# Attention kernel: 256-column q and k products issued one at a time between 512-column products

## The chip, the cores and the metric

The kernel runs on one core of one Trainium2 chip. The metric is the device time of one execution in microseconds (us); the time of a kernel is the median of several runs. The engines are named as the profile names them: PE is TensorE's matmul, PEld its weight load, DVE is VectorE, ACT is ScalarE, POOL is GpSimd, SP is SyncE.

## The reference, cut to what matters

```python
# x: (4, 64, 64, 256); Wq, Wk: (256, 128); Wv: (256, 256); gamma: one number
q = einsum('bwhc,cd->bwhd', x, Wq) + bq
k = einsum('bwhc,cd->bwhd', x, Wk) + bk
v = einsum('bwhc,cd->bwhd', x, Wv) + bv
pq, pk, pv = q.reshape(B, -1, N), k.reshape(B, -1, N), v.reshape(B, -1, N)   # N = 4096
energy = einsum('bcn,bcm->bnm', pq, pk)          # contraction over 128
attention = softmax(energy, axis=-1)
out = einsum('bcm,bnm->bcn', pv, attention)
return gamma * out.reshape(B, W, H, C) + x
```

For each of the 4 images there are 4096 positions; the score matrix is 4096 x 4096 and is never kept whole.

## The kernel before, in words

All products are float32. To keep precision at the rate of single products, each operand is split into a rounded upper part `h`, a rest `l` and a combination `d`, and each exact product is made of three matmuls over these forms (form numbers 0, 1 and 2; 2 is `d`). Every matmul here has 128 stationary columns and streams 512 or 256 moving columns.

**The main loop** (`for n in range(B * STEPS)`) takes 512 units of work, 128 for each image: 8 groups of 512 output columns by 16 steps over the keys. One unit issues, in this order of the program, which is also the order on each engine (the schedule is written by hand):

1. `cross(n + LOOK)`: two matmuls of form 2 into the two score banks (L378), each followed on ACT by a scaling in place (L379).
2. `step(p, "act")`: ACT's share of the preparation of the next image.
3. `attend(n, 0)`: six matmuls (L452) that add v times attention to the first half's two accumulators: two with `h`, two with `l`, two with `d`.
4. `energy(n + LOOK)`: four matmuls (L393), two for each score bank, each pair followed on ACT by an exponential (L396).
5. `load_k`, `store`, and `upper` on ACT (L402).
6. `step(p, "pe")`: PE's share of the preparation of the next image.
7. `halves(n + 1)` on DVE: the running sum (L413), then `l` (L428) and `d` (L430) of the next unit; then `step(p, "dve")`: DVE's share of the preparation.
8. `attend(n, 1)`: six matmuls (L452) for the second half.

So a unit has 18 matmuls of 512 columns on PE, and those of the preparation when the unit has some.

**The preparation of the next image** (`step`, images 1 to 3) goes in periods of R = 16 units. Each period makes q, k and v of two blocks of 256 positions, `i` and `i + 1`, at the place `r` in the period:

- r = 1, 2 (DVE): each block of x is transposed into a spare PSUM bank (p0 or p1).
- r = 3, 4 (ACT, then DVE, L165): the transposed block's `h`, then `d` (tile `xd`) and `l` (tile `xf`). The `l` is the last reader of the bank.
- r = 5 (PE, L267): `products(b, i, 0, (2,))` and the same for `i + 1`, 4 + 4 matmuls of 256 columns with `xd`, into p0 and p1. Then DVE scales these banks and adds the bias (`seed_qk`, L295).
- r = 6 (PE, L267): `products(b, i, 0, (0, 1))` and the same for `i + 1`, 8 + 8 matmuls of 256 columns with `xf`.
- r = 7, 8 (ACT, L317) and r = 7 to 10 (DVE, L320): the forms of q and k of `i`, then of `i + 1`, stored to DRAM.
- r = 9 to 14: the same for v, in products of 512 columns (`products_v`, L284), which take p0 at r = 9 and p1 at r = 11.

There are 8 periods in each of images 1 to 3, so 24 in all; in image 0 the products are made ahead of the main loop, by the same function.

Of the kernel before, what the change touches and what calls it, by code (L numbers as in the profile page):

```python
# [20 lines left out]
def kernel(  # L21
# [79 lines left out]
    with ExitStack() as fast:  # L101
# [41 lines left out]
        nc.gpsimd.dma_start(gam, gamma.partition_broadcast(P))  # L143

        qd, kf, vf, units, loads, now = {}, {}, {}, {}, {}, {}
        active, stores, xloads = [], [], []

        def proceed():
            for pieces in list(active):
# [38 lines left out]
        def bank(name, shape, b, ring):  # L188
            if b:
                tile_ = spare(name, shape)  # L190
                now["turn"] += 1
                return tile_
            pool, tag = next(rings[ring])
            return pool.tile(shape, F32, tag=tag, name=name)
# [52 lines left out]
            units["xf", b, i] = f  # L247
            yield from split(*f, y, b == 0 and i > 1)

        def products(b, i, w, fs):  # L250

            xf = units["xf", b, i]
            if fs[0] == 2:
                ring = 1
                if b == 0 and w and i >= NI - 2:
                    ring = 0
                    next(rings[1])
                units[w, b, i] = bank(f"qv{w}_{b}_{i}", [P, 2, C], b, ring)
            to = units[w, b, i]
            for s in range(2):  # L260
                for f in fs:
                    for k in range(KC):
                        if w:
                            left, right = wf[:, 1, f, k, s * P : (s + 1) * P], xf[f][:, k]
                        else:
                            left, right = xf[f][:, k, s, :], wf[:, 0, f, k]
                        nc.tensor.matmul(  # L267
                            to[:, s, :],
                            left,
                            right.rearrange("p s a -> p (s a)") if w else right,  # L270
                            start=(f == 2 and s == k == 0),
                            stop=(f == 1 and k == KC - 1),
                            skip_group_check=True,
                        )

        def products_v(b, i, eh, fs):

# [15 lines left out]
        def seed_qk(b, i):  # L293
            y = units[0, b, i]
            nc.vector.scalar_tensor_tensor(  # L295
                y, y, REST, bias.unsqueeze(1).to_broadcast([P, 2, C]), ALU.mult, ALU.add
            )
# [8 lines left out]
        def seed_v_pair(b, i, eh):  # L306
            y = units["v", b, i, eh]
            nc.scalar.activation(y, y, AF.Identity, bias=bvs[:, eh : eh + 1], scale=REST)
# [52 lines left out]
        def load_k(n):  # L361
            b, u = divmod(n, STEPS)
            if b < B:
                t = kpool.tile([P, 2, 3, P], F32R, tag="k", name=f"k_{b}_{u}")
                nc.gpsimd.dma_start(t, kf[b, u % NU])  # L365
                loads["k", n] = t

        def forms(n, i, f):
            b, u = divmod(n, STEPS)
            return loads["k", n][:, i, f, :], loads["q", b, u // NU][:, :, f, :]  # L370

        def cross(n):

            if n >= B * STEPS:
                return
            for i in range(2):
                e = units["e", n, i] = ps_e.tile([P, NB], F32, tag="e", name=f"e_{n}_{i}")
                nc.tensor.matmul(e, *forms(n, i, 2), start=True, stop=False, skip_group_check=True)  # L378
                nc.scalar.mul(e, e, -REST)  # L379

        def energy(n):

            if n >= B * STEPS:
                return
            if n % NU:
                x = ppool.tile([P, 2, NB], F32, tag="x", name=f"x_{n}")
            else:
                x = ppool.tile([P, 2, NB], F32, tag="s", name=f"s_{n // NU}")
            units[n] = x
            for i in range(2):  # L390
                e = units.pop(("e", n, i))
                for f in range(2):
                    nc.tensor.matmul(  # L393
                        e, *forms(n, i, f), start=False, stop=(f == 1), skip_group_check=True
                    )
                nc.scalar.activation(x[:, i, :], e, AF.Exp, scale=(1.0 + E) ** 3 / E)  # L396

        def upper(n):
# [41 lines left out]
        def attend(n, j, order=(0, 1, 2)):  # L440

            t = n % NU
            if t == 0:
                for i, c in enumerate("ab"):
                    pool, tag = ps_o, f"{c}{j}"
                    if j and n >= (B - 1) * STEPS and n // NU % 2 == 0:
                        pool, tag = now["banks"][i]
                    now[c, j] = pool.tile([P, NB], F32, tag=tag, name=f"{c}{j}_{n // NU}")
            for f in order:
                to = now["ab"[f == 2], j]  # L450
                for i in (1, 0) if f == 1 else (0, 1):
                    nc.tensor.matmul(  # L452
                        to,
                        vall[:, t, i, f, j * P : (j + 1) * P],
                        units[n][f][:, i, :],
                        start=(t == 0 and i == 0 and f != 1),
                        stop=(t == NU - 1 and f != 0 and i == f // 2),
                        skip_group_check=True,
                    )

        def emptied(n, j, banks=None, only=None, vector=False):

# [100 lines left out]
        def step(n, engine):  # L563

            if n < 0:
                return
            b, u = divmod(n, STEPS)
            i, r = divmod(u, R)
            b, i = b + 1, 2 * i
            if b >= B:  # L570
                return
            made = now["made"]

            def begin(key, pieces):
                made[key] = pieces
                next(pieces)

            if engine == "pe":
                if r == 5:
                    products(b, i, 0, (2,))  # L580
                    products(b, i + 1, 0, (2,))
                elif r == 6:
                    products(b, i, 0, (0, 1))
                    products(b, i + 1, 0, (0, 1))
                elif r in (9, 11):
                    products_v(b, i, r // 11, (2,))
                elif r in (10, 12):
                    products_v(b, i, r // 12, (0, 1))
            elif engine == "act":
                if r in (3, 4):  # L590
                    begin(("x", r - 3), x_forms(b, i + r - 3))
                elif r in (7, 8):
                    begin(("qk", r - 7), qk_forms(b, i + r - 7))
                elif r in (10, 12):
                    seed_v_pair(b, i, r // 12)
                    if r == 12:
                        load_x(b + (i + 2) // NI, (i + 2) % NI)
                elif r in (11, 13):
                    begin(("v", r // 13), v_pair_forms(b, i, r // 13))
            else:  # L600
                if r in (1, 2):
                    transposed(b, i + r - 1)
                elif r in (3, 4):
                    next(made["x", r - 3])
                    next(made["x", r - 3])
                elif r == 5:
                    seed_qk(b, i)
                    seed_qk(b, i + 1)
                elif 7 <= r <= 10:
                    next(made["qk", (r - 7) // 2])  # L610
                    if r % 2 == 0:
                        next(made["qk", (r - 7) // 2], None)
                elif 11 <= r <= 14:
                    next(made["v", (r - 11) // 2])
                    if r % 2 == 0:
                        next(made["v", (r - 11) // 2], None)
# [84 lines left out]
        for n in range(B * STEPS):  # L701
            b, u = divmod(n, STEPS)
# [7 lines left out]
            if n == B * STEPS - 6:  # L710
                xr = ppool.tile([P, 2, NB], F32, tag="s", name="xr")
                nc.sync.dma_start(xr, xg[b, g])
            cross(n + LOOK)
            turn = t == NU - 1 and not final
            if t == 0 and n:
                upper(n + LOOK - 1)
            p = n - 2 + (n > 17)
            step(p, "act")
            late = n >= (B - 1) * STEPS
            if not final:  # L720
                attend(n, 0)
            if late and 1 <= t <= 2 and n > 1:
                emptied(n - 1 - t, 1, done, t - 1)
            energy(n + LOOK)
            load_k(n + LOOK + 3)
            store()
            if t == 0 and n:
# [22 lines left out]
            for m in range(2 * NU):  # L750
                c, r = divmod(n + NU - 3 - 13 * m // 16, STEPS)
# [11 lines left out]
    with tc.If(nc.values_load(again[0:1, 0:1]) > 0), ExitStack() as general:  # L763
# [91 lines left out]
        for b in range(B):  # L855
# [16 lines left out]
            for g in range(NG):  # L872
                ps = []
                mx = work.tile([P, 2, NB], F32, tag="mx", name=f"gmx_{b}_{g}")
                for t in range(NP):
# [9 lines left out]
                    p = ppool.tile([P, 2, NB], F32, tag="p", name=f"gp_{b}_{g}_{t}")  # L885
# [52 lines left out]
                r = work.tile([P, NB], F32, tag="r", name=f"gr_{b}_{g}")  # L938
# [36 lines left out]
```

## Time and profile before

| | |
|---|---|
| median of 3 runs | 2300.16 us (2299.88 to 2301.19) |
| the profiled execution's own time | 2299.82 us |
| span in the profile, first to last instruction | 2298.0 us |
| mean granted TensorE clock | 0.999 |
| PE busy | 2286.8 us, 10566 matmuls |
| DVE busy | 2160.6 us |
| ACT busy | 1794.3 us |
| 256-column products in images 1 to 3 | 576 (192 with `xd`, 384 with `xf`) |

The profiled execution lies 0.34 us below the median of the runs, and 1.8 us of it lie outside the span. In the rows of a timeline the columns are the start in us from the span's start, the length in us, engine, line, operation, output and inputs, and how many equal instructions were merged. A matmul's length includes the way through the array, and matmuls overlap; what one of them costs PE is the distance from its start to the start of the next.

### The profile page before, as it was taken

The page shows a single profiled execution, that of the slowest core. Times are in us where ns is not written, and L with a number is a line of the kernel's source. Part 1 is how long each engine was busy: PE and PEld are TensorE (multiplying, and loading weights), DVE is VectorE, ACT ScalarE, POOL GpSimd, SP SyncE. Part 2 cuts the span into 40 slices and gives each one's busy share as a digit, 9 for nine tenths or more (in the row PEclk, how much of TensorE's full clock was granted, in tenths as well). Part 3 has the DMA queues.
Part 4 walks back from the last instruction along what each step waited for, and adds up shares of the span by engine and source line. Part 5 has one row for each costly group of instructions (what it writes and reads, how often), then busy time and mean ns, then how long its engine had stood idle before and what let it go on. Part 6 is the DMA issues. An engine that isn't in the chain of part 4 may idle for free.

```text
span 2298.0 us, 31903 instructions
## 1 busy us (share of the span) xinstructions
PE 2286.8 (100%) x10566; PEld 1912.7 (83%) x10566; DVE 2160.6 (94%) x2222; ACT 1794.3 (78%) x2917; POOL 445.3 (19%) x747
## 2 busy tenths in 40 slices
PE   9999999999999999999999999999999999999998
PEld 9888888888888888888888888888888888888886
DVE  8999999999999999999999999999999899888888
ACT  7778777787777877777777778777788777888885
POOL 7111111111231111111122111111112211111110
PEclk9999999999999999999999999999999999999999
DMA  8567766677996777666799667766689855555554
GB/s 272 161 172 212 195 180 165 174 210 194 279 278 194 196 195 192 181 167 184 209 301 278 180 178 206 199 177 170 169 228 299 243 148 144 136 137 146 151 142 107
DMA packets 305727, 445.31 MB, mean 194 GB/s; under 512 B 129682, under 2 KB 183188, under 8 KB 305556
## 3 DMA queue, kind: packets, MB, share of 16 engines
q0 software_dynamic: 105584, 296.79, 49.5%
q1 hardware_dynamic: 199424, 146.14, 20.6%
q8 instruction: 87, 1.43, 0.3%
q14 instruction: 84, 0.69, 0.1%
q10 hardware_dynamic: 548, 0.26, 0.0%
HBM read 313.79 MB, written 112.26 MB: 185 GB/s over the span
## 4 chain that ended last, share of the span: by engine, by line
PE 99%; DVE 0%; ACT 0%; DMA 0%; issue 0%; DVEq 0%
PE a L452 40%; PE e L393 20%; PE b L452 20%; PE e L378 10%; PE qv L267 5%; PE v L284 3%; PE xt L229 0%; DMA xs<-in_x_dram 0%; ACT qv L302 0%; DVE ld L430 0%; PE wp L140 0%; PE zp L525 0%; DVE o_last L555 0%; DVE o_last L550 0%; DVE o_last L556 0%
## 5 line engine op out<-in xcount | busy, mean ns | idle before, releaser
L396 ACT ACTIVATE x<-e 128x512 f32<-128x512 f32 x960 | 522.0, 596 | 324.1 <-PE e L393 324.1
L379 ACT ACTIVATE e<-e 128x512 f32<-128x512 f32 x1024 | 546.3, 570 | 114.8 <-PE e L378 114.8
L452 PE MATMUL a<-h,v 128*128 128x512 f32 x2048 | 631.3, 389 | 0.0
L452 PE MATMUL b<-ld,v 128*128 128x512 f32 x2048 | 631.0, 389 | 0.1
L452 PE MATMUL a<-ld,v 128*128 128x512 f32 x2048 | 630.9, 389 | 0.0
L413 DVE TENSOR_TENSOR s<-s,x 128x1024 f32<-128x1024 f32 x480 | 585.2, 1219 | 48.3 <-ACT x L396 46.7
L365 POOL DMA_DIRECT2D k<-kf x512 | 273.0, 533 | 1799.9 <-PE e L393 1750.1
L428 DVE TENSOR_TENSOR ld<-x,h 128x1024 fp32r<-128x1024 f32 x480 | 585.6, 1220 | 22.6 <-ACT h L402 22.2
L430 DVE SCALAR_TENSOR_TENSOR ld<-h,x 128x1024 fp32r<-128x1024 f32 x480 | 585.8, 1220 | 0.0
L393 PE MATMUL e<-q,k 128*128 128x512 f32 x2048 | 547.6, 389 | 0.0
L402 ACT ACTIVATE h<-x 128x1024 fp32r<-128x1024 f32 x480 | 510.8, 1064 | 14.2
L452 PEld LDWEIGHTS b<-ld,v 128*128 128x128 f32 x2048 | 384.2, 188 | 80.9 <-DVE ld L430 1.1
L452 PEld LDWEIGHTS a<-ld,v 128*128 128x128 f32 x2048 | 384.5, 188 | 80.3
L393 PEld LDWEIGHTS e<-q,k 128*128 128x128 f32 x2048 | 384.4, 188 | 79.6
L452 PEld LDWEIGHTS a<-h,v 128*128 128x128 f32 x2048 | 381.4, 188 | 75.9
L378 PE MATMUL e<-q,k 128*128 128x512 f32 x1024 | 315.4, 389 | 0.0
L378 PEld LDWEIGHTS e<-q,k 128*128 128x128 f32 x1024 | 192.0, 188 | 39.9
L320 DVE SCALAR_TENSOR_TENSOR f<-f,qv 128x512 fp32r<-128x512 f32 x128 | 86.2, 684 | 0.3
L267 PE MATMUL qv<-wf,xf 128*128 128x256 f32 x576 | 77.2, 285 | 0.6 <-DVE qv L295 0.4
L267 PEld LDWEIGHTS qv<-wf,xf 128*128 128x128 f32 x576 | 73.7, 191 | 3.6 <-DVE qv L295 0.6
L428 DVE TENSOR_TENSOR ld<-s,h 128x1024 fp32r<-128x1024 f32 x32 | 39.3, 1227 | 37.0 <-ACT h L402 34.4
L165 DVE SCALAR_TENSOR_TENSOR vf<-vf,v 128x512 fp32r<-128x512 f32 x96 | 65.6, 683 | 0.0
(87 smaller groups left out, 1100.3 us busy)
## 6 DMA issues: line engine op xcount, KB each, us to landing
k<-kf POOLq DMA_DIRECT2D x512, 384.0 KB, 3.7
vf<-vf SPq DMA_DIRECT2D x96, 384.0 KB, 4.8
v<-vf POOLq DMA_DIRECT2D x96, 384.0 KB, 6.0
kf<-f SPq DMA_DIRECT2D x128, 192.0 KB, 3.9
qd<-f SPq DMA_DIRECT2D x124, 192.0 KB, 3.9
q<-qd POOLq DMA_DIRECT2D x31, 768.0 KB, 5.2
o<-o POOLq DMA_DIRECT2D x31, 512.0 KB, 5.3
o<-in_x_dram POOLq DMA_DIRECT2D x31, 512.0 KB, 6.8
```

The costliest lines, as they stand in the source:

```text
L267: nc.tensor.matmul(to[:, s, :], left, right.rearrange("p s a -> p (s a)") if w else right, start=(f == 2 and s == k == 0), stop=(f == 1 an ...
L320: nc.vector.scalar_tensor_tensor(f[:, :, :, j, :], h.bitcast(F32), s, y, ALU.mult, op)
L365: nc.gpsimd.dma_start(t, kf[b, u % NU])
L378: nc.tensor.matmul(e, *forms(n, i, 2), start=True, stop=False, skip_group_check=True)
L379: nc.scalar.mul(e, e, -REST)
L393: nc.tensor.matmul(e, *forms(n, i, f), start=False, stop=(f == 1), skip_group_check=True)
L396: nc.scalar.activation(x[:, i, :], e, AF.Exp, scale=(1.0 + E) ** 3 / E)
L402: nc.scalar.activation(h, units[n], AF.Identity, scale=UPPER)
L413: nc.vector.tensor_tensor(s, s, x, ALU.add)
L428: nc.vector.tensor_tensor(l, x, h.bitcast(F32), ALU.subtract)
L430: nc.vector.scalar_tensor_tensor(d, h.bitcast(F32), 1.0 + E, x, ALU.mult, ALU.subtract)
L452: nc.tensor.matmul(to, vall[:, t, i, f, j * P : (j + 1) * P], units[n][f][:, i, :], start=(t == 0 and i == 0 and f != 1), stop=(t == NU - ...
```

## The change

The function `products` becomes a generator, `each_product`, that yields after each matmul. A list `between` holds generators that wait to be emitted; `mix()` emits one matmul of the first of them, and `flush()` all that are left. `mix()` is called after each matmul of `cross` and `energy`, and after each of `attend` except the two with `h` of the first half.

The 8 products with `xd` at r = 5 are put on the list ahead of `attend(n, 0)` (a new engine name, "first"): 4 fall between the `l` and `d` matmuls of `attend(n, 0)`, 4 between those of `energy`. The 8 products of block `i` with `xf` are put on the list at r = 6, after `energy`, and fall between the 6 matmuls of `attend(n, 1)` and the 2 of the next unit's `cross`. The 8 of block `i + 1` do the same at r = 7, one unit later than before. `flush()` stands after `cross` and after `energy`. Image 0's products keep their runs. The other engines' instructions keep their order.

```diff
+        def mix():
+            while between:
+                if next(between[0], None) is None:
+                    del between[0]
+                else:
+                    return
+
+        def flush():
+            while between:
+                mix()
+
+        def products(*which):
+            for _ in each_product(*which):
+                pass
+
-        def products(b, i, w, fs):
+        def each_product(b, i, w, fs):
...
                             skip_group_check=True,
                         )
+                        yield True
...
                 nc.tensor.matmul(e, *forms(n, i, 2), start=True, stop=False, skip_group_check=True)
+                mix()
                 nc.scalar.mul(e, e, -REST)
...
                         e, *forms(n, i, f), start=False, stop=(f == 1), skip_group_check=True
                     )
+                    mix()
...
                         stop=(t == NU - 1 and f != 0 and i == f // 2),
                         skip_group_check=True,
                     )
+                    if j or f:
+                        mix()
...
-            if engine == "pe":
+            if engine == "first":
                 if r == 5:
-                    products(b, i, 0, (2,))
-                    products(b, i + 1, 0, (2,))
-                elif r == 6:
-                    products(b, i, 0, (0, 1))
-                    products(b, i + 1, 0, (0, 1))
+                    between.append(each_product(b, i, 0, (2,)))
+                    between.append(each_product(b, i + 1, 0, (2,)))
+            elif engine == "pe":
+                if r in (6, 7):
+                    between.append(each_product(b, i + r - 6, 0, (0, 1)))
...
             cross(n + LOOK)
+            flush()
...
             if not final:
+                step(p, "first")
                 attend(n, 0)
...
             energy(n + LOOK)
+            flush()
```

More of the change, by code (lines that the diff above doesn't have):

```diff
@@ L145 @@
         qd, kf, vf, units, loads, now = {}, {}, {}, {}, {}, {}
-        active, stores, xloads = [], [], []
+        active, stores, xloads, between = [], [], [], []
         def proceed():
```

## The prediction

> **What bounds the kernel now.** I read the page first: busy times, then the chain that ended last.
>
> ```profile
> span 2298.0 us, 31903 instructions
> PE 2286.8 (100%) x10566; PEld 1912.7 (83%) x10566; DVE 2160.6 (94%) x2222; ACT 1794.3 (78%) x2917; POOL 445.3 (19%) x747
> ...
> PE 99%; DVE 0%; ACT 0%; DMA 0%; issue 0%; DVEq 0%
> ```
>
> PE is the chain: 99% of the span is one matmul after another. A busy PE need not be an efficient one, so the next question is how far apart the matmuls start. The waits of PE come next, all that the view lists:
>
> ```profile
> engine line waited for: us in total, times, longest us
> PE wp L140 <- DVE ones L132: 1.1, 1, 1.1
> PE qv L267 <- DVE qv L295: 0.4, 1, 0.4
> PE xt L229 <- DMA xs<-in_x_dram: 0.3, 1, 0.3
> PE qv L267 <- ACT qv L302: 0.2, 1, 0.2
> ```
>
> They come to 2.0 us and stand at the beginning. There is nothing to win from waits: only a matmul's own cost counts, and any new wait of PE adds to the time in full.
>
> Then PE's timeline over one period's products (r = 5 to 8), where a start minus the start before it is what the matmuls between them cost:
>
> ```profile
> start us, us, engine line op out<-in xcount [idle before <-releaser]
> ...
> 799.43 0.62 PE L452 MATMUL a<-h,v 128*128 128x512 f32 x2
> ...
> 800.79 1.07 PE L393 MATMUL e<-q,k 128*128 128x512 f32 x4
> 801.70 1.11 PE L267 MATMUL qv<-wf,xd 128*128 128x256 f32 x8
> 802.65 0.63 PE L452 MATMUL a<-h,v 128*128 128x512 f32 x2
> 803.12 0.62 PE L452 MATMUL a<-ld,v 128*128 128x512 f32 x2
> 803.58 0.62 PE L452 MATMUL b<-ld,v 128*128 128x512 f32 x2
> 804.03 0.61 PE L378 MATMUL e<-q,k 128*128 128x512 f32 x2
> 804.49 0.62 PE L452 MATMUL a<-h,v 128*128 128x512 f32 x2
> ...
> 806.75 2.08 PE L267 MATMUL qv<-wf,xf 128*128 128x256 f32 x16
> 808.67 0.63 PE L452 MATMUL a<-h,v 128*128 128x512 f32 x2
> ...
> 810.51 0.62 PE L452 MATMUL a<-h,v 128*128 128x512 f32 x2
> ...
> 814.59 0.62 PE L452 MATMUL a<-h,v 128*128 128x512 f32 x2
> ```
>
> The unit from 810.51 to 814.59 has no 256-column product: 4.08 us for 18 matmuls, **226.7 ns** each. The unit at 799.43 has 8 and takes 5.06 us, so they cost 0.98 us; the one at 804.49 has 16 and takes 6.02 us, so 1.94 us. The difference, 0.96 us for 8, gives **120 ns** for one more product in a run. Half a 512-column matmul would be 113.3 ns. The rest, 0.98 - 8 x 0.12 = 0.02 us, is paid once a run, and the rows show where: the matmuls after the run start 0.47, 0.46, 0.45 us apart by pairs instead of 0.453, and the eight from 802.65 to 804.49 take 1.84 us instead of 1.813. The two runs of a period cost 2.92 us for 24 products, **121.7 ns** each.
>
> The same timeline at single points inside the first run (the first row of each answer is the matmul then running, merged with the next):
>
> ```profile
> 801.70 0.40 PE L267 MATMUL qv<-wf,xd 128*128 128x256 f32 x2
> ```
>
> ```profile
> 801.81 0.40 PE L267 MATMUL qv<-wf,xd 128*128 128x256 f32 x2
> ```
>
> ```profile
> 801.93 0.40 PE L267 MATMUL qv<-wf,xd 128*128 128x256 f32 x2
> ```
>
> The first product, the one that follows a 512-column matmul, costs 0.11 us; the others (0.95 - 0.11) / 7 = 0.12 us. So the price grows inside the run: the second product already finds PE behind. The weight loads say the same from the other side, in the groups of lines L267 and L452 from 70 us on (lengths in ns: least, median, most):
>
> ```profile
> L267 PEld LDWEIGHTS qv<-wf,xf x384: 187/192/192, 101.4 to 1730.4; 128*128 128x128 f32 x192
> L267 PE MATMUL qv<-wf,xf x384: 277/283/283, 101.6 to 1730.5; 128*128 128x256 f32 x192
> L267 PEld LDWEIGHTS qv<-wf,xd x192: 187/192/192, 96.4 to 1724.4; 128*128 128x128 f32 x192
> ```
>
> ```profile
> L452 PEld LDWEIGHTS a<-ld,v x2042: 187/188/188, 71.7 to 2288.5; 128*128 128x128 f32 x186
> ```
>
> A load between 512-column matmuls takes 187 to 188 ns; in a run of 256-column ones its median is 192. Loads crowd in the runs and not elsewhere. Their own rate is not shown anywhere, so that a run is held up by them is my reading, not a measurement.
>
> **The change part by part.** *Removed:* 48 runs in 24 periods, 24 x 2.92 = 70.1 us. *Added:* the same 576 products (384 + 192 in the rows), each between two 512-column matmuls. The trace has no such place, so the price is bounded. From below: half of a 512-column matmul, 113.3 ns, with which the first product of a run agrees (0.11). From above: a run's price of 120 ns and the whole 0.02 us that returning to 512 columns costs, 140 ns. I take 113.3, the row nearest to the new place: that first product also follows a 512-column matmul, and whatever follows it needs a weight load of the same size. Then 576 x 113.3 ns = 65.3 us, and the sum is 65.3 - 70.1 = **-4.8 us**. I count no tail after a single product, since the second product of a run starts on time and the crowding shows only from then on.
>
> *The Trainium skill* would have it otherwise. "TensorE: Matmul & The Clock Gate", section "Back-to-back issue gap", gives a warm matmul a gap of N / 2.4 + 2.5 ns, and section "LDWEIGHTS (loading the stationary operand)" gives 106.7 ns for 128 columns, less than that gap for N = 256 (109.2). By it a run is not held up by loads, and an estimate from that page would leave nothing for the change to remove. The trace disagrees with the gap itself (226.7 ns against 215.8 for 512 columns, 120 against 109.2 for 256), so I keep the rows, and its sense as a rival below.
>
> *Moved, r = 5:* the `xd` products go ahead, past half of `attend(n, 0)`. PE is in order, so whatever such a product waits for holds up the scores and the sums behind it. The fourth product of `i` is done before `energy`; the first of `i + 1` comes after the first `energy` matmul and needs the bank that `xf`'s `l` form reads last. DVE's timeline there, and around the next unit but one:
>
> ```profile
> 797.66 1.22 DVE L430 SCALAR_TENSOR_TENSOR ld<-h,x 128x1024 fp32r<-128x1024 f32 x1
> 798.79 0.68 DVE L165 SCALAR_TENSOR_TENSOR xd<-xf,xt 128x512 fp32r<-128x512 f32 x1
> 799.39 0.68 DVE L165 SCALAR_TENSOR_TENSOR xf<-xf,xt 128x512 fp32r<-128x512 f32 x1
> ...
> 802.26 1.22 DVE L430 SCALAR_TENSOR_TENSOR ld<-h,x 128x1024 fp32r<-128x1024 f32 x1
> ```
>
> ```profile
> 808.70 1.22 DVE L430 SCALAR_TENSOR_TENSOR ld<-h,x 128x1024 fp32r<-128x1024 f32 x1
> ```
>
> The `l` is done at 800.07. PE comes to that product at 799.43 + 7 x 0.2267 + 4 x 0.1133 = 801.47: 1.4 us to spare. Without that cover the price would be the lateness itself, once a period.
>
> *Moved, r = 6 and 7:* 8 products leave r = 6, so unit r = 7 starts its `attend(n, 0)` about 1 us earlier: at 799.43 + 2 x (18 x 0.2267 + 8 x 0.1133) = 809.40 instead of 810.51. Its first `d` matmul comes four later, at 810.31; DVE's `d` is done at 808.70 + 1.22 = 809.92. The slack shrinks from 1.5 to 0.4 us and holds: nothing. If it did not, each 0.1 us would be 2.4 us over 24 periods. The bias on p0 and p1 (L295) comes behind the 802.26 row on DVE, after 803.48, when the products are long done. Block `i + 1` ends in the next `cross`, just ahead of ACT's reading of it at r = 8, where ACT first has the two scalings to do, 570 ns each:
>
> ```profile
> L379 ACT ACTIVATE e<-e 128x512 f32<-128x512 f32 x1024 | 546.3, 570 | 114.8 <-PE e L378 114.8
> ```
>
> A product behind the second `cross` matmul takes 0.11 us, within them. The DMA issues, SP's and POOL's queues keep their order; the stores of `i + 1` hang on the forms at r = 9 and 10, as before. Nothing.
>
> *The first period* is different: there DVE is late already.
>
> ```profile
> 94.34 0.61 PE L452 MATMUL a<-ld,v 128*128 128x512 f32 x2
> 95.09 0.73 PE L452 MATMUL b<-ld,v 128*128 128x512 f32 x2
> ```
>
> ```profile
> 93.80 1.23 DVE L430 SCALAR_TENSOR_TENSOR ld<-h,x 128x1024 fp32r<-128x1024 f32 x1
> ...
> 95.53 0.69 DVE L165 SCALAR_TENSOR_TENSOR xf<-xf,xt 128x512 fp32r<-128x512 f32 x1
> ```
>
> PE stands 0.3 us for `d` (95.09 - 94.34 - 2 x 0.2267), into which two products now fit (-0.2 us); the bank of `i + 1` is read until 96.22 and wanted at 95.09 + 3 x 0.2267 + 2 x 0.1133 = 96.00 (+0.2 us). Together nothing.
>
> So 2299.82 - 4.8 = 2295.0 us for an execution like the profiled one, which lies 0.34 us under the median of the runs: **2295.4 us** expected.
>
> **The rivals.**
>
> *The price goes with the instruction, not with its neighbours.* 226.7 - 120 = 106.7 ns for 256 columns more: taken so, each matmul has a fixed 13.3 ns, and 120 is what a 256-column one costs anywhere. For it: two rows fit with one constant, and the skill's rule above has this form. Against it: the first product's 0.11. Only the 48 x 0.02 us go: -1.0 us, 2299.2 us. The same comes out if a single product costs 113.3 and the 512-column one behind it 6.7 more.
>
> *The return to 512 columns is paid each time: slower.* The 0.02 us come after 8 as after 16 products, so a single one may cost them in full. Place: the first 512-column matmuls behind each product; price 140 ns, 576 x (140 - 121.7) = +10.6 us, 2310.8 us. It decides from 121.7 ns a product on, that is if more than 8 of the 20 ns, added to 113.3, come with each single one. For it: the slower matmuls go on over 1.8 us behind a run, longer than the distance between two single products. Against it: they follow runs in which PE has fallen behind. Half of it would be about 2301.
>
> *DVE's `d` at r = 7 is late.* With 0.4 us used up, each 0.2 us beyond is 4.8 us and cancels the gain: 2300. Against it: DVE waits for nothing new.
>
> *The change doesn't come about* can be left out: with 6 + 2 and 4 + 4 places for 8 products, nothing is left for `flush()` to issue in a run.
>
> **How the numbers follow.** Single products at 113 ns or a little less: 0.48. Its -4.8 us is just past 0.2% (4.6 us), which is about what a measurement of this kernel can tell from no change; I give 0.34 to faster, since the first product's 0.11 allows a price under 113.3 too, and 0.14 to no change. The fixed price, and the gain cancelled by late DVE: 0.26, no change. The paid return: 0.26, of it 0.21 slower and 0.05 no change. So faster 0.34, no change 0.45, slower 0.21. The range goes from 2293.5 (110 ns a product, the first one's 0.11 taken as it stands: 576 x 11.6 ns = 6.7 us under 2300.16) to 2306.0 (132 ns a product, most of a paid return). It takes in the fixed price and the cancelled gain; left out are the full return, about 0.14, and less than 110 ns, 0.04.
>
> **What would show it.** Right: in the profile after, an `attend` with products between its matmuls advances by 0.34 us for each pair (226.7 + 113.3); the units at r = 5, 6 and 7 take 4.99 us each; the loads of L282 (L267 before) drop to 188 ns. If the pairs take 0.347 us, the price is fixed; if 0.36, the return is paid, and the rows behind show it. A wait of PE for DVE at r = 5 or 7, some 20 times, would show a slack that I misjudged. The prediction is wrong if the 0.11 us of a first product were borrowed from those behind it.

## The result: slower by 0.28%

| | before | after |
|---|---|---|
| median | 2299.91 us (2299.83 to 2301.19, 9 runs) | 2306.25 us (2306.04 to 2308.26, 9 runs) |
| the profiled execution's own time | 2299.82 us | 2306.27 us |
| span | 2298.0 us | 2304.5 us |

The ratio is 1.0028, with a 95% interval from 1.0018 to 1.0038: 6.3 us more (2306.25 - 2299.91). The prediction was 2295.4 us, in a range from 2293.5 to 2306.0: the change went the other way, and the time lies 0.25 us above the range.

The page of the changed kernel, the lines on the busy engines and on the chain:

```profile
PE 2293.0 (100%) x10566; PEld 1911.3 (83%) x10566; DVE 2162.9 (94%) x2222; ACT 1799.0 (78%) x2917; POOL 445.5 (19%) x747
...
PE 99%; DVE 0%; ACT 0%; DMA 0%; issue 0%; DVEq 0%
```

PE has as many matmuls as before and is still the chain; it is busy 6.2 us longer. The granted clock is 0.999 in both, so the clock is not what differs. So the same matmuls cost more, or PE waits for something that counts as busy. Its waits, the one line that was not there before:

```profile
PE qv L282 <- DVE xf L165: 0.2, 1, 0.2
```

One wait, once. The time is in the matmuls, and PE's timeline shows it. First unit r = 5, of which the rows with the 8 `xd` products are left out; then r = 6, from 380.29, and the start of r = 7, at 385.37:

```profile
375.16 0.61 PE L470 MATMUL a<-h,v 128*128 128x512 f32 x2
...
380.29 0.62 PE L470 MATMUL a<-h,v 128*128 128x512 f32 x2
...
382.79 0.28 PE L282 MATMUL qv<-wf,xf 128*128 128x256 f32 x1
382.90 0.40 PE L470 MATMUL a<-h,v 128*128 128x512 f32 x1
383.13 0.28 PE L282 MATMUL qv<-wf,xf 128*128 128x256 f32 x1
383.25 0.40 PE L470 MATMUL a<-ld,v 128*128 128x512 f32 x1
383.49 0.28 PE L282 MATMUL qv<-wf,xf 128*128 128x256 f32 x1
383.61 0.40 PE L470 MATMUL a<-ld,v 128*128 128x512 f32 x1
383.85 0.28 PE L282 MATMUL qv<-wf,xf 128*128 128x256 f32 x1
...
385.37 0.64 PE L470 MATMUL a<-h,v 128*128 128x512 f32 x2
385.85 0.63 PE L470 MATMUL a<-ld,v 128*128 128x512 f32 x2
386.32 0.62 PE L470 MATMUL b<-ld,v 128*128 128x512 f32 x2
```

The units r = 5 and 6 are 5.13 and 5.08 us long instead of the 4.99 forecast; r = 7 takes 5.14 (the next unit's first row is at 390.51). Inside them, take the distances between starts. A product costs 0.11 or 0.12 us, as hoped. But the 512-column matmul behind it costs 0.23 or 0.24: from 382.79 to 383.85 three products and three 512-column matmuls take 1.06 us, 0.353 a pair, where 0.227 + 0.113 = 0.340 was forecast. And after the last product the 512-column matmuls stay slow for a while: 0.48 and 0.47 us by pairs instead of 0.453.

### The profile page after: what moved, and what is told of

The parts are those of the page before. It is cut to its first block, busy times and chain, and to the rows that moved or that the text cites. A ratio compares the mean times of both kernels' runs of the same rounds, so it can differ in the third digit from the quotient of the medians.

```text
span 2304.5 us, 31927 instructions
## 1 busy us (share of the span) xinstructions
PE 2293.0 (100%) x10566; PEld 1911.3 (83%) x10566; DVE 2162.9 (94%) x2222; ACT 1799.0 (78%) x2917; POOL 445.5 (19%) x747
## 4 chain that ended last, share of the span: by engine, by line
PE 99%; DVE 0%; ACT 0%; DMA 0%; issue 0%; DVEq 0%
PE a L470 40%; PE e L410 20%; PE b L470 20%; PE e L394 10%; PE qv L282 5%; PE v L300 3%; PE xt L229 0%; DMA xs<-in_x_dram 0%; ACT qv L318 0%; DVE xf L165 0%; PE zp L545 0%; DVE o_last L575 0%; DVE o_last L570 0%; DVE qv L311 0%; DVE o_last L576 0%
## 5 line engine op out<-in xcount | busy, mean ns | idle before, releaser
L470 PE MATMUL a<-ld,v 128*128 128x512 f32 x2048 | 641.2, 390 | 0.0
L470 PE MATMUL b<-ld,v 128*128 128x512 f32 x2048 | 641.0, 390 | 0.0
L470 PE MATMUL a<-h,v 128*128 128x512 f32 x2048 | 638.2, 390 | 0.0
L410 PE MATMUL e<-q,k 128*128 128x512 f32 x2048 | 557.9, 390 | 0.0
L394 PE MATMUL e<-q,k 128*128 128x512 f32 x1024 | 321.8, 390 | 0.0
L282 PE MATMUL qv<-wf,xf 128*128 128x256 f32 x576 | 135.1, 283 | 0.7 <-DVE qv L311 0.4
L282 PEld LDWEIGHTS qv<-wf,xf 128*128 128x128 f32 x576 | 96.9, 189 | 4.0 <-DVE qv L311 0.6
L165 DVE SCALAR_TENSOR_TENSOR vf<-vf,v 128x512 fp32r<-128x512 f32 x96 | 65.3, 680 | 0.0
```

The lines of the kernel that those rows point to most:

```text
L282: nc.tensor.matmul(to[:, s, :], left, right.rearrange("p s a -> p (s a)") if w else right, start=(f == 2 and s == k == 0), stop=(f == 1 an ...
L410: nc.tensor.matmul(e, *forms(n, i, f), start=False, stop=(f == 1), skip_group_check=True)
L470: nc.tensor.matmul(to, vall[:, t, i, f, j * P : (j + 1) * P], units[n][f][:, i, :], start=(t == 0 and i == 0 and f != 1), stop=(t == NU - ...
```

## The experiments

A row of matmuls is called settled here when its starts are equally far apart: 226.7 ns for 512 float32 columns. **Theory R**: PE itself pays for coming back to 512 columns, whenever it has done something narrower. This payment is called a return. **Rival W**: the moved work pays, through waits, semaphores or other engines in the kernel.

**PE alone** (`pe_patterns`). A kernel of its own: it copies x to the output, computes no attention, and issues rows of matmuls of the same shapes; once its data is there, at 16 us, PE has nothing to wait for. `pattern(n, m, times)` is n products of 256 columns, then m of 512, so often; `calm()` is 30 of 512.

```diff
+    for n in (1, 2, 3, 4, 6, 8, 16, 32):
+        pattern(n, 0, 1)
+        calm()
+    for n, m, times in ((1, 1, 8), (1, 1, 24), (1, 2, 16), ..., (1, 12, 8), (2, 1, 12), ...):
+        pattern(n, m, times)
+        calm()
+    pattern(1, 1, 24, same=True)      # all into one bank
...
+    pattern(24, 0, 1, src=half)       # bfloat16
+    calm(30, half)
+    pattern(1, 1, 24, src=half)
```

> This kernel leaves the attention out: it copies x and runs matmuls alone, float32 as in the kernel, 256-column products among 512-column ones in many patterns, with no wait, and its time means nothing. Theory R (the return to 512 columns is paid by PE itself): one 512-column and one 256-column product in turn take 353 ns, as in the trace of the changed kernel, and a run of 8 among 512-column products costs 980 ns, as in the trace before; a lone product far from others costs 127 to 140 ns. Rival W (waits, semaphores or the other engines in the kernel slow the singles): in turn they take 340 to 347 ns here, where nothing waits. Rival H (float32 alone): the same patterns in bfloat16 take the sum of their two steady prices, with no extra.

PE's timeline of this kernel; `slim` are the products, `wide` the 512-column matmuls:

```profile
28.36 0.28 PE L45 MATMUL slim<-data 128*128 128x256 f32 x1
28.47 6.99 PE L45 MATMUL wide<-data 128*128 128x512 f32 x30
35.30 0.40 PE L45 MATMUL slim<-data 128*128 128x256 f32 x2
...
64.38 1.12 PE L45 MATMUL slim<-data 128*128 128x256 f32 x8
...
72.16 2.08 PE L45 MATMUL slim<-data 128*128 128x256 f32 x16
...
91.56 0.28 PE L45 MATMUL slim<-data 128*128 128x256 f32 x1
...
101.23 0.28 PE L45 MATMUL slim<-data 128*128 128x256 f32 x1
...
209.90 2.91 PE L45 MATMUL wide<-data 128*128 128x512 f32 x12
212.76 2.91 PE L45 MATMUL wide<-data 128*128 128x512 f32 x12
```

From 28.36 to 35.30 are one product and 30 of 512 columns: 6.94 - 30 x 0.2267 = **0.14 us** for the one. Of it 0.11 stand before the next start, and 0.03 are spread over the matmuls behind. Eight cost 72.16 - 64.38 - 6.80 = 0.98. For 1, 2, 3, 4, 6, 8, 16 and 32 the trace gives 120 ns a product and the same 20 ns once. One product every 12 matmuls, 209.90 to 212.76, costs 2.86 - 12 x 0.2267 = 0.14 again. The 8 in turn begin at 91.56, and at 101.23, 8 products and 38 of 512 columns later, they have cost 9.67 - 8.61 = 1.06 us, 132 ns each. That is the changed kernel's pattern, with no wait of PE and no other engine at work. So PE alone repeats the loss, and W is not needed for it. The same kernel also puts 24 products in turn into the accumulator bank of the 512-column matmuls between them. With the 30 of 512 behind them these take 15.28 us, and as long with a bank of their own (101.23 to 116.51), so a change of bank is not what is paid for.

In bfloat16 nothing is paid:

```profile
460.15 0.27 PE L45 MATMUL slim<-half 128*128 128x256 bf16 x1
...
467.62 0.27 PE L45 MATMUL slim<-half 128*128 128x256 bf16 x1
```

Between these rows stand 23 pairs in turn, 7.47 / 23 = 0.325 us each: 215.7 + 109, what a row of each alone costs there.

**In the kernel: five other ways to place the same products.** What each would cost by R follows from the returns; a period of before has 2.

*Runs of 8* (`runs_of_8`): block i + 1 keeps its later unit, and nothing is put singly.

```diff
...
-                if r in (6, 7):
-                    between.append(each_product(b, i + r - 6, 0, (0, 1)))
+                if r == 5:
+                    products(b, i, 0, (2,))
+                    products(b, i + 1, 0, (2,))
+                elif r in (6, 7):
+                    products(b, i + r - 6, 0, (0, 1))
```

> The products stand in runs again, but block i + 1 keeps its later unit: three runs of 8 a period. Theory R: 3 x 0.98 = 2.94 us a period instead of 2.92, so +0.5 us over before (2300.4). Rival W by the moved block (its forms and stores come later, r = 7 starts earlier): most of the +6.3 us stays.

*Only the `xd` products singly* (`singles_d_only`):

```diff
-                if r in (6, 7):
-                    between.append(each_product(b, i + r - 6, 0, (0, 1)))
+                if r == 6:
+                    products(b, i, 0, (0, 1))
+                    products(b, i + 1, 0, (0, 1))
```

> Only the 8 products with xd at r = 5 are put singly; the 16 with xf are one run at r = 6 as before. Theory R: a third of the loss, 24 x (8 x 132.9 - 980) ns = +2.0 us (2301.9). Rival W by DVE's lateness at r = 5: nearly all of +6.3 us. Rival W by the moved block: nothing, 2299.9.

*Two at a time* (`pairs`) and *four at a time* (`fours_close`), in the singles' places:

```diff
         def mix():
+            for _ in range(2):      # 4 in fours_close
-            while between:
+                while between:
...
```

> Two 256-column products at a time between 512-column ones, in the same units as the singles: 12 returns a period instead of 24. Theory R: a period costs 24 x 120 ns and 13 to 20 ns a return, 3.04 to 3.12 us, so +2.8 to +4.8 us over before (2302.7 to 2304.7). If the price goes with the number of places used and not with returns, it lies half way, +3.2. Rival W: +6 us as with singles.

> Four products, one 512-column matmul, four products, in the places of the singles; 6 returns a period, 3 of them at once followed by products. Theory R: a return that is cut short after one matmul costs at most 6.7 to 13 ns instead of 20, so 3 x 20 + 3 x (3 to 13) ns, 2.95 to 2.98 us a period, +0.7 to +1.4 us over before (2300.8 to 2301.5), less than the fours apart. Rival (price by places used): +1.9.

*Four at a time, far apart* (`fours_apart`): no `mix()` in `cross`, `energy` or `attend`; four products ahead of `attend(n, 1)`, four behind it, in units r = 5, 6 and 7. The bias of block i + 1 moves to r = 6.

```diff
...
+                if r == 5:
+                    products(b, i, 0, (2,))
+                    between.append(each_product(b, i + 1, 0, (2,)))
-                if r in (6, 7):
+                elif r in (6, 7):
                     between.append(each_product(b, i + r - 6, 0, (0, 1)))
+                    for _ in range(4):
+                        mix()
...
             attend(n, 1)
+            flush()
```

> Six runs of 4 a period, each at least 6 matmuls of 512 columns from the next; block i + 1 has its bias added one unit later. Theory R: 24 x 120 + 6 x 20 ns = 3.00 us a period, so +1.9 us over before (2302.0), as much as the pairs with 12 returns close together gave. Rival (the price goes with the number of products that stand alone): nothing stands alone, so +0.7 us as with runs of 8.

The intervals of the ratios are about 0.2% wide, too wide for steps of 0.02%. The trace resolves them: in each kernel the first `xd` product of one period and that of the period 20 later. In the order before, after, runs of 8, only `xd`, pairs, fours close, fours apart:

```profile
234.34 1.12 PE L267 MATMUL qv<-wf,xd 128*128 128x256 f32 x8
...
1652.73 1.12 PE L267 MATMUL qv<-wf,xd 128*128 128x256 f32 x8
```

```profile
233.48 0.28 PE L282 MATMUL qv<-wf,xd 128*128 128x256 f32 x1
...
1657.07 0.28 PE L282 MATMUL qv<-wf,xd 128*128 128x256 f32 x1
```

```profile
235.90 1.11 PE L282 MATMUL qv<-wf,xd 128*128 128x256 f32 x8
...
1654.69 1.11 PE L282 MATMUL qv<-wf,xd 128*128 128x256 f32 x8
```

```profile
235.10 0.28 PE L282 MATMUL qv<-wf,xd 128*128 128x256 f32 x1
...
1655.10 0.28 PE L282 MATMUL qv<-wf,xd 128*128 128x256 f32 x1
```

```profile
233.51 0.40 PE L283 MATMUL qv<-wf,xd 128*128 128x256 f32 x2
...
1653.11 0.40 PE L283 MATMUL qv<-wf,xd 128*128 128x256 f32 x2
```

```profile
235.17 0.64 PE L283 MATMUL qv<-wf,xd 128*128 128x256 f32 x4
...
1653.97 0.64 PE L283 MATMUL qv<-wf,xd 128*128 128x256 f32 x4
```

```profile
234.57 0.64 PE L282 MATMUL qv<-wf,xd 128*128 128x256 f32 x4
...
1654.57 0.64 PE L282 MATMUL qv<-wf,xd 128*128 128x256 f32 x4
```

The distance over 20 is the length of a period:

| kernel | period, us | over before, ns | by R, ns | x 24, us | median over before's on the same chip, us | ratio, 95% interval |
|---|---|---|---|---|---|---|
| before | 70.92 | | | | | |
| after (singles) | 71.18 | 260 | 3 x 1060 - 2920 = 260 | 6.2 | 6.3 | 1.0028 (1.0018 to 1.0038) |
| runs of 8 | 70.94 | 20 | one return more, 20 | 0.5 | 0.7 | 1.0002 (0.9993 to 1.0011) |
| only `xd` singly | 71.00 | 80 | 1060 - 980 = 80 | 1.9 | 1.75 | 1.0006 (0.9997 to 1.0015) |
| pairs | 70.98 | 60 | 120 to 200 | 1.4 | 2.2 | 1.0009 (1.0000 to 1.0018) |
| fours close | 70.94 | 20 | 30 to 60 | 0.5 | 1.5 | 1.0007 (0.9998 to 1.0016) |
| fours apart | 71.00 | 80 | four returns more, 80 | 1.9 | 1.9 | 1.0008 (0.9998 to 1.0017) |

Where returns stand alone, R is exact to the resolution: 20 ns each, for runs of 8 as for fours apart. The rival "what stands alone pays" falls with the fours apart, where nothing stands alone and 80 ns are paid. The singles' loss at r = 5 alone is a third of the whole and no more. Pairs and fours close came out cheaper than expected: my guess of 13 to 20 ns for a return that is cut short was too high.

Three medians lie above 24 periods' worth: by 0.2 us (runs of 8), 0.8 (pairs) and 1.0 (fours close). The traces show where, if the start of each `attend` matmul is compared with that of the same one in before. Against the settled periods, the first period adds 0.5 us in pairs and 0.8 in fours close, where PE stands for DVE's `l` of the transposed block, as the lists of waits show:

```profile
PE qv L283 <- DVE xf L165: 0.7, 1, 0.7
```

```profile
PE qv L283 <- DVE xf L165: 0.9, 1, 0.9
```

The second period adds 0.25 us in each of these two and 0.3 in runs of 8: unit r = 7 has come forward, and its `d` is not ready. In runs of 8 PE reaches it at 172.97 + 2 x 0.2267 = 173.42, and DVE ends it at 172.29 + 1.22 = 173.51:

```profile
172.29 1.22 DVE L448 SCALAR_TENSOR_TENSOR ld<-h,x 128x1024 fp32r<-128x1024 f32 x1
```

```profile
172.97 0.61 PE L470 MATMUL a<-ld,v 128*128 128x512 f32 x2
173.56 0.74 PE L470 MATMUL b<-ld,v 128*128 128x512 f32 x2
```

The start at 173.56 is late by 0.14 us, too little for the list of waits, and the two matmuls from there take 0.58 us instead of 0.453 (the next row is at 174.14). So W is there too, but in the first two periods alone: in the changed kernel it is 0.1 us of the 6.3.

**What disturbs the row?** (`pe_patterns_2`, again without the attention.)

```diff
+    for width, src in ((256, half), (512, half), (128, data), (64, data)):
+        narrow(1, width, src, False)
+        calm()
+    one(512, slim[1])
+    nc.scalar.activation(slim[1], slim[1], AF.Identity, scale=0.5)
+    one(512, slim[1])
+    calm()
...
+    # and the stop with bfloat16 on both sides
```

> Leaves the attention out, as the first pattern kernel did. Theory R (a settled row of float32 512-column matmuls has a rhythm, and finding it again costs 20 ns): 8 in turn cost 132.6 ns a product as before, four pairs with one 512-column matmul between them far less than 4 x 20 ns extra, 2 x 8 apart by 16 the full 2 x 20. If what must be found again is the rhythm and not the width, a lone 512-column matmul in bfloat16, a 128-column one and a stop of PE for ACT are each followed by the same 233, 236, 228 ns. Rival (the width itself, 256 against 512): only the narrower ones are, and a stop or a bfloat16 one of 512 columns is followed by 227 at once.

PE's timeline: a stop of PE for ACT among float32 matmuls, then one among bfloat16 ones.

```profile
166.46 0.50 PE L45 MATMUL slim<-data 128*128 128x512 f32 x1 [0.67 <-ACT slim L76]
166.80 7.02 PE L45 MATMUL wide<-data 128*128 128x512 f32 x30
173.66 0.39 PE L45 MATMUL slim<-data 128*128 128x512 f32 x1
...
198.56 0.38 PE L45 MATMUL slim<-half 128*128 128x512 bf16 x1 [0.67 <-ACT slim L82]
198.77 6.63 PE L45 MATMUL wide<-half 128*128 128x512 bf16 x30
205.24 1.04 PE L45 MATMUL slim<-half 128*128 128x256 bf16 x8
```

After the stop the first float32 matmul costs 0.34 us to the next start, and the 30 behind it take 6.86 us instead of 6.80, though all are 512 wide; in bfloat16 it is 0.21 and 6.47, 215.7 ns each, with nothing extra. After two stops in a row the 30 float32 ones lost 0.03 us. The lone bfloat16 matmul of 512 columns, the 128-column and the 64-column one were each followed by slower starts too. So it is not the narrow width alone: each of these breaks the settled row of float32 512-column matmuls, and it costs tens of ns until the row is settled again. The even distance of a settled row is called its rhythm here. Two runs of 8 with 16 matmuls between them paid a full return each, 1.96 us for 16 products. The first two patterns of this kernel, with the order of the pairs and the fours close, cost 0.992 and 0.981 us for 8 products. Three times that, less the 2.92 us of before, makes about 60 and 20 ns a period, as in the table.

**Whose rhythm?** (`pe_columns`, without the attention.) The same rows with fewer stationary columns.

```diff
-        nc.tensor.matmul(to[:, :width], w, m[:, :width], ...
+        nc.tensor.matmul(to[:c, :width], w[:, :c], m[:, :width], ...      # c = 128, 96, 64, 32
```

> Leaves the attention out, as the other pattern kernels. The same matmuls with 128, 96, 64 and 32 stationary columns, so that each weight load brings fewer columns and the moving side stays as it is. If the rhythm is one of weight loads beside the moving stream, the 13.3 ns over the columns' own time in the steady rows and the 20 ns of a return shrink with the columns, at 32 to a few ns; if it belongs to the moving stream alone, 226.7, 120 and 20 ns stay at every number of columns.

The weight loads by form, mean ns behind the bar, and the timeline (30 matmuls, then 8 products):

```profile
L47 PEld LDWEIGHTS wide<-data 128*128 128x128 f32 x244 | 46.5, 192 | 25.3 <-ACT data L31 15.5
...
L47 PEld LDWEIGHTS wide<-data 128*32 128x32 f32 x168 | 18.3, 109 | 20.0
```

```profile
37.39 6.99 PE L47 MATMUL wide<-data 128*128 128x512 f32 x30
44.21 1.11 PE L47 MATMUL slim<-data 128*128 128x256 f32 x8
...
167.49 7.10 PE L47 MATMUL wide<-data 128*32 128x512 f32 x30
174.42 1.09 PE L47 MATMUL slim<-data 128*32 128x256 f32 x8
```

Neither answer came. The loads get shorter, from 192 to 109 ns, and the 512-column matmuls dearer: 6.93 us for 30 with 32 columns, 231 ns, against 6.82 with 128 (the 0.02 of a return included). Fewer columns never settle at 226.7; they stay at 230 to 231 in a pattern that repeats. The products go the other way. The last five of the 8, with 128 columns and with 32:

```profile
44.56 0.76 PE L47 MATMUL slim<-data 128*128 128x256 f32 x5
```

```profile
174.78 0.73 PE L47 MATMUL slim<-data 128*32 128x256 f32 x5
```

The next 512-column matmuls start at 45.16 and 175.35, so five products take 0.60 us with 128 columns and 0.57 with 32: 120 and 114 ns each. So neither price is the time of the moving columns and a fixed rest, and what sets the rhythm stays open.

## Why the prediction was wrong, point by point

- *PE is the chain and the waits are nothing*: right before, and after but for the first two periods.
- *A run costs 120 ns a product and 0.02 us once*: right, and PE alone repeats it from 1 to 32 products.
- *"I take 113.3, the row nearest to the new place"* and *"I count no tail after a single product"*: this is the step that failed. The first product of a run does cost 0.11 to the next start, alone as well; but the 0.02 us of the run's end are not the run's. They belong to the return, and a lone product pays 140 ns in full, 27 of them in the rows behind it. The prediction named this as what would make it wrong. Its term for the added products, 65.3 us, measures 576 x 132.5 ns = 76.3. In close order the return is cut short by the next product, so that 8 in turn pay 132 ns each instead of 140: 576 x (132.5 - 121.7) ns = 6.2 us more, not 4.8 less.
- *"Loads crowd in the runs", a run is held up by them*: the forecast that loads drop to 188 ns came true, and the time rose all the same:

```profile
L282 PEld LDWEIGHTS qv<-wf,xf x384: 187/188/190, 101.8 to 1742.6; 128*128 128x128 f32 x192
```

  So the length of a load does not tell what its product costs. The reading itself, that a run is held up by its loads, stays open: with 32 stationary columns a load takes 109 ns and a product inside a run 114 instead of 120, but the 512-column matmuls get dearer, and no run separates the loads from what else goes with the columns.
- *DVE's slack at r = 5 and r = 7*: held from the third period on. For the first, "together nothing" was right: the wait of 0.2 us is in the list, PE's older loss there shrinks in turn, and the period costs the same 0.26 us more as the others. In the second, which the prediction did not single out, the `d` of r = 7 is late, for 0.1 us.
- *The rivals*: the paid return was right in mechanism and place and too dear by 7.5 ns a product (2310.8; measured 2306.25). I gave it 0.26 and the range half of it. What spoke for it stood in the rows: 0.02 us after 8 as after 16 means that the number of products doesn't matter, and then nothing makes 1 an exception. I set that aside for one interval of 0.11, which says when the next matmul starts and not what the whole costs. The fixed price is right for every run (226.7 - 120 ns for 256 columns more) and lacks the return.
- *The rule of the Trainium skill* ("TensorE: Matmul & The Clock Gate", section "Back-to-back issue gap"), N / 2.4 + 2.5 ns: in bfloat16 the trace agrees, 215.7 and 109 ns for 512 and 256 columns, alone and in turn. In float32 it does not: the gaps are 226.7 and 120 ns, and wider behind a disturbance. That a run is not held up by loads was the prediction's inference from it; the runs leave that open.

A version faster than both was not found. By an estimate from the return of 20 ns, one run of 24 a period would save 0.5 us in all, less than a measurement of this kernel can tell; it was not run, since DVE's bias stands between the two runs.

## What to carry to other kernels

Where PE never waits, the price of a matmul is what the whole row gains when it is taken out, and not the distance to the next start: measure from a settled row to a settled row. An extra that is the same after 8 and after 16 points to a price for each change, and then fewer and longer runs are cheaper, and spreading them is dearer. A pattern kernel of a few hundred matmuls can test this without the rest of the kernel; here 8 products in turn cost 1.06 us, a third of the 3.18 that the 24 of a period cost in the changed kernel.

## What the runs showed of the hardware that I had not expected

- Float32 matmuls of 128 x 512 settled at 226.7 ns only where nothing else was among them; a lone 256-column one costs 140 ns, 20 ns more than it does in a row of its own. In bfloat16 the prices add up.
- Two 512-column matmuls after each product are no better than one: 16 products with two between them cost 0.134 us each, 24 with one between them 0.127, 8 so 0.132. A lone product every 12 costs its full 0.14, and pairs in turn with one between them 0.121.
- After a stop of PE the next 30 float32 matmuls took 0.06 us more than a settled row (0.03 after two stops); nothing of the kind shows in bfloat16.
- With 32 stationary columns instead of 128 a float32 matmul of 512 columns is slower, 231 ns against 226.7, and one of 256 columns in a run quicker, 114 against 120.
